# A four-layer image network on one core: moving layer 3's tile copies off GpSimd, shifting its gate chain, and reordering the loads at the start

## The chip, the core and the metric

The kernel runs on one core of a Trainium2 chip. The metric is the time of one execution in microseconds on the device, from its start to its end, as the median of several runs. A core has five engines that run side by side, each through its own queue of instructions in order: TensorE (PE, matrix products; its weight loads are listed as PEld), VectorE (DVE), ScalarE (ACT), GpSimd (POOL) and SyncE (SP, which here only issues transfers). ACT's queue issues transfers as well. SBUF is the working memory. Matrix products land in PSUM[...].

## The reference, cut to what matters

The input `x` is (4, 256, 48, 48): four samples, 256 channels, 2304 pixels. Four layers are applied in turn.

```python
# layer 0: group norm of x, then attention with 8 heads of 64 over all 2304
#          pixels; q and k are normed to length 1, scale 10; x = x + w_out(o)
# layer 1: group norm; gate from max-pool, blur-pool and depthwise 11x3 / 3x11
#          convolutions; x = x + norm * gate
# layer 2: group norm; non-local block: theta, phi, g of 64 channels each,
#          y = softmax(theta^T phi) g; W y goes through a batch norm over all
#          four samples; x2 = x + that
# layer 3: group norm of x2 -> h
#          gate = sigmoid(W2 leaky(W1 mean(h)))        one number per channel
#          z = depthwise 3x3 convolution of (h * gate) + bias
#          x = x2 + leaky(instance_norm(z))                leaky: slope 0.01
```

All data is float32. Layer 3's batch norm needs statistics over all samples, so nothing of layer 3 can start before the last attention unit of layer 2 is done.

## The kernel before, in words

`usual_path` (L56 to L1885) does the whole network; a second path further down is a fallback that doesn't run. Three samples' `x` live in SBUF as tiles of 128 partitions x 2 halves of the channels (k = 0, 1) x 2304 pixels. Sample 0's `x` is parked in DRAM before layer 3 and shares the buffer of sample 1.

**Start.** `load_x` brings in the first sample. The transfers of small parameters are issued on ACT's queue (L121 to L148): the vectors `vec`, then eleven weights of layers 2 and 3 (`w2c`, `b2c`, `Ww`, `w1`, `w2`), then `wo`. Behind them on ACT stands a one-element Exp (L168), which makes ACT load its table. `gn(0, ..., first=True)` takes `bn_stats` of each 384-column slice on DVE (L194), and reduces over groups with matrix products against the constant `gmat` (L215, L225). A reciprocal square root is done on POOL (`rsqrt`, L179). `norms` folds the normalization into the projection weights: PE computes bias vectors (L549) and ACT scales the weights in two 128x384 operations (L556). `start` projects (L581).

**Attention.** `attend()` (L454) runs phases of units; a unit is a run of key tiles, with two score products (L290), an exponential on ACT (L296), and two value products (L310) in each slot. Other work is put into numbered slots by a `work` dictionary and by `others`, lists of closures that are spread over slots: `spread(work, closures, slots)`. At the end of a unit the row sums are made (L399), inverted (`reciprocal`, L404) and multiplied in. `note(u)` (L407) keeps extremes of the row sums, from which `judge` decides at the end whether the usual path's results can be used. In layer 2, `w_mul` (L1087) forms W y in PSUM and `bn_stats` (L1095, L1369) takes its statistics; `sample_means(b)` aggregates them for each sample (L1139) and `earlier(k)` merges the first three samples. The next sample's group norm and its six projection chunks (`project2`, L1035 to L1056) are also spread over slots, and follow the statistics there.

**Layer 3.** Here all five queues run in the order in which the code is written (`manual_schedule`, L1400). PSUM is split into one `w` tile of two banks and three `cv` tiles of two banks. The samples are taken in the order `SEQ = [1, 2, 3, 0]`; a tile is one sample's one channel half, so there are eight tiles, and each has six conv steps (slices of 384 pixels). A tile i passes through these stages:

- `w_product(i, c)` (L1449): PE forms W y for one third of the pixels, into a PSUM tile of two banks.
- `grow(i, c)` (L1502): DVE scales it, adds x, and writes x2 into a padded image (50 x 50 with a border). Two operations, one for each bank.
- `square(i, c)` (L1526): ACT sums the squares around the mean. `border(i)` (L1511, L1514): POOL fills the frame.
- `place(i, h, j, q, how)` (L1535): copies 32 channels of half an image (32x1298) into `shifted`, moved by one of the taps' offsets. Each half tile needs twelve of them. Eight cross partitions (`AWAY`) and go through SP's queue as transfers. Four (j = q) stay in their partitions and are copies on an engine: L1542 on ACT, L1544 on POOL, L1546 on DVE.
- `products` (L1659): PE's convolution, twelve matrix products in each step, with taps on 96 or 128 rows.
- `evict` (L1671) and `square` (L1682): ACT takes the results to SBUF with their sums. `moments`, `scales`, `shift` (L1690 to L1730): DVE makes scale and shift, with one `rsqrt` on POOL.
- `scale` (L1736, ACT), `leak` (L1742, DVE: leaky relu), `gain` (L1747, DVE: adds x2), `store` (L1753, SP). Each has three pieces of 768 pixels a tile.

The class `Chain` computes one sample's gate in nine small operations: `total` (L1579, DVE), `groups` (L1586, PE), `inverse` (L1590, DVE, then POOL), `pooled` (L1596, DVE), `first_layer` (L1601, PE), `hidden` (L1608, DVE), `second_layer` (L1615, PE), `gate` (L1622, ACT), `scaled` (L1626, DVE). Its three matrix products write into the same `w` tile as the x2 products.

The order is set by an event table: `at(t, rank, fn)` puts a closure at conv step t, and within a step closures go out in the order of their ranks (FRONT, CONV, PRODUCT, GROW, MID, EVICT, SMALL, MOMENTS, SQUARE, SCALE, LAST, PLACE, STORE). `put_before` places the products and grows of a tile in the steps t-12 to t-10, if its conv starts at t; `put_tile` places conv and what follows it; `put_chain(t, steps)` places a gate chain at offsets from t, the first step of a sample. The last tile's statistics are taken straight from PSUM, and its scale, leak and gain come after the table, together with the pieces that `late` has collected from the tile ahead of it.

## Time and profile before

| | us |
|---|---|
| median of three runs | 3552.23 |
| lowest, highest run | 3548.91, 3552.97 |
| the profiled execution | 3548.99 |
| its span, from the first to the last instruction | 3547.2 |
| first projection matmul (L581) | 18.02 |
| last layer-2 row sums (L399) | 3358.37 |
| first conv step of layer 3 (L1659) | 3387.28 |
| last DVE operation (L1747) | 3540.55 |

A profile's line gives the line of the program, the engine, the operation and `out<-in` with shapes. In a list of groups there follow the count, the busy time, the mean of one in nanoseconds, and the idle time ahead of it with what ended it ("12.0 <-DVE pad L1502" is 12.0 us of waiting that VectorE's writing of `pad` ended). In a timeline, each line begins with the start and the length in microseconds of a run of like instructions, and ends with the idle time ahead of it. One float32 matrix product of the program appears as two records. A view by windows gives, for stretches of time, how long each engine was busy in them.

From 3357 to 3541 us, the groups that the change touches are these:

| row | count | busy us | mean ns |
|---|---|---|---|
| L1659 PE conv | 1152 | 105.6 | 512 |
| L1542 ACT copy 32x1298 | 26 | 33.0 | 1269 |
| L1544 POOL copy 32x1298 | 39 | 54.2 | 1389 |
| L1502 DVE grow 128x384 from the w tile | 38 | 21.6 | 611 |
| L1747 DVE gain 128x768 | 24 | 28.0 | 1166 |
| L1742 DVE leak 128x768 | 24 | 25.4 | 1057 |
| L1449 PE x2 product to the w tile | 152 | 17.6 | 536 |

Ten more grow operations and 40 more product records work on cv tiles, at the start of layer 3.

### The profile page before, as it was taken

To read this page: it belongs to the slowest core of one execution; us is meant where nothing else is said; L and a number is where in the kernel's file an instruction comes from. 1 tells how busy PE (TensorE), PEld (TensorE's weight loads), DVE (VectorE), ACT (ScalarE), POOL (GpSimd) and SP (SyncE) were. 2 spreads that over 40 slices of the span, in tenths; PEclk is the share of its full clock that TensorE was granted. 3 is DMA by queue.
4 is the path that set the end of the run, shared out by engine and by line. 5 is a ranking of instruction groups with operands and counts; after the bars stand their busy time and mean duration, and the time that the engine had idled before them with its cause. 6 is when DMAs were issued, how large, how long until landed. Compare 5 with 4: busy or idle time off the path is not lost. (4 is left out here: it accounts for less than half of the span.)

```text
span 3547.2 us, 88373 instructions
## 1 busy us (share of the span) xinstructions
PE 3426.8 (97%) x37036; PEld 1727.0 (49%) x37036; DVE 2550.9 (72%) x3472; ACT 2380.1 (67%) x3847; POOL 818.5 (23%) x626
## 2 busy tenths in 40 slices
PE   8999999999999999999999999999999999898976
PEld 4554545554444444444444444444444445565422
DVE  3455555567788788687887886878878879655856
ACT  4665666665886796558867975579668755555476
POOL 2333333321101010000111001110100116665553
PEclk9999999999999999999999999999999999999988
DMA  2211111111111111221111111111111100000076
GB/s 94 48 26 22 26 22 26 22 26 22 22 26 22 26 22 26 56 45 21 26 20 26 21 26 22 26 22 26 22 22 22 22 8 6 6 7 6 4 187 186
DMA packets 121752, 116.61 MB, mean 33 GB/s; under 512 B 58832, under 2 KB 112704, under 8 KB 120576
## 3 DMA queue, kind: packets, MB, share of 16 engines
q1 hardware_dynamic: 118592, 108.70, 16.4%
q8 instruction: 292, 4.78, 0.6%
q10 hardware_dynamic: 2752, 2.17, 0.2%
q14 instruction: 116, 0.95, 0.1%
HBM read 56.99 MB, written 11.80 MB: 19 GB/s over the span
## 5 line engine op out<-in xcount | busy, mean ns | idle before, releaser
L296 ACT ACTIVATE pt<-sc 128x768 f32<-128x768 f32 x1944 | 1475.2, 811 | 729.7 <-PE sc L290 721.2
L336 DVE TENSOR_TENSOR acc<-acc,pt 128x768 f32<-128x768 f32 x1368 | 1368.9, 1001 | 172.9 <-ACT pt L296 72.8
L310 PE MATMUL av<-pt,v 64*64 64x384 f32 x13824 | 1274.7, 484 | 0.0
L290 PE MATMUL sc<-q,k 64*64 64x384 f32 x13824 | 1269.9, 482 | 0.5 <-ACT pt L296 0.5
L290 PEld LDWEIGHTS sc<-q,k 64*64 64x64 f32 x13824 | 525.2, 133 | 589.7 <-issue 543.4
L310 PEld LDWEIGHTS av<-pt,v 64*64 64x64 f32 x13824 | 518.0, 133 | 599.1 <-issue 566.0
L391 POOL TENSOR_TENSOR o<-o,rinv 128x384 f32<-128x384 f32 x95 | 114.6, 1206 | 1737.3 <-DMA rinv<-rinv 1737.3
L321 POOL TENSOR_TENSOR half<-pt 128x768 f32<-128x768 f32 x189 | 364.1, 1930 | 539.4 <-ACT pt L296 502.3
L336 DVE TENSOR_TENSOR acc<-acc,half 128x768 f32<-128x768 f32 x171 | 192.8, 1127 | 232.6 <-POOL half L321 231.6
L677 DVE SCALAR_TENSOR_TENSOR x<-pj,bo,x 128x384 f32<-128x384 f32 x192 | 118.4, 617 | 308.6 <-PE pj L664 307.2
L853 ACT ACTIVATE prod<-pd,wt 128x256 f32<-128x256 f32 x486 | 337.0, 764 | 0.2
L581 PE MATMUL pj<-xs,w 128*128 128x384 f32 (+1 forms) x720 | 275.4, 505 | 0.0
L581 PEld LDWEIGHTS pj<-xs,w 128*128 128x128 f32 x720 | 124.1, 189 | 127.9 <-issue 39.5
L310 PE MATMUL av<-pt,qv 64*64 64x384 f32 x1728 | 177.0, 498 | 0.0
L290 PE MATMUL sc<-qv,kd 64*64 64x384 f32 x1728 | 171.4, 485 | 2.4 <-ACT pt L296 2.4
L876 DVE TENSOR_REDUCE prod<-prod 128x256 f32<-128x1280 f32 x114 | 168.7, 1480 | 0.3 <-ACT prod L853 0.3
L664 PE MATMUL pj<-o,wo 128*128 128x384 f32 (+1 forms) x384 | 159.8, 499 | 5.7 <-issue 3.6
L612 PEld LDWEIGHTS pj<-w,xs 128*128 128x128 f32 x1080 | 134.5, 191 | 24.1 <-issue 1.2
L612 PE MATMUL pj<-w,xs 128*128 128x128 f32 x1080 | 134.9, 275 | 0.0
L387 POOL TENSOR_TENSOR o<-raw 128x384 f32<-128x384 f32 x95 | 124.4, 1309 | 43.3 <-ACT raw L383 43.2
L330 DVE TENSOR_TENSOR acc<-pt 128x768 f32<-128x768 f32 x99 | 115.5, 1166 | 26.1 <-ACT pt L296 26.1
L383 ACT COPY raw<-av 128x768 f32<-128x768 f32 x108 | 86.4, 800 | 48.0 <-PE av L310 45.6
(247 smaller groups left out, 2402.4 us busy)
## 6 DMA issues: line engine op xcount, KB each, us to landing
xs<-in_x_dram SPq DMA_DIRECT2D x90, 384.0 KB
sh<-pad SPq DMA_DIRECT2D x126, 162.2 KB
rinv<-rinv SPq DMA_DIRECT2D x208, 94.5 KB
out_dram<-x SPq DMA_DIRECT2D x24, 384.0 KB
l<-row SPq DMA_DIRECT2D x416, 1.5 KB
w<-in_wqkv_dram SPq DMA_DIRECT2D x32, 192.0 KB
x<-in_x_dram SPq DMA_DIRECT2D x4, 1152.0 KB
x<-in_x_dram SPq DMA_DIRECT2D x9, 384.0 KB
```

The lines of the kernel that those rows point to most:

```text
L290: nc.tensor.matmul(ps[c * D : (c + 1) * D, h, :SL], lhsT=u["of"]["k"][r, j0 : j0 + D], rhs=u["of"]["q"][r, u["qc"]], start=True, stop=True,)
L296: nc.scalar.activation(pt, ps[:, :, :SL], AF.Exp, scale=u["scale"])
L310: nc.tensor.matmul(u["av"][h * D : (h + 1) * D, half, :SL], lhsT=value(u, j, h)[r], rhs=pt[r, h, :], start=j == 0, stop=j == JB - 1,)
L321: nc.gpsimd.tensor_add(half, pts[0], pts[1])
L336: nc.vector.tensor_add(u["acc"], u["acc"], term)
L387: eng.tensor_add(u["sum"], u["raw"][:, 0, :], u["raw"][:, 1, :])
L581: nc.tensor.matmul(ps[:, :n], lhsT=at["w"][:, k, t, :], rhs=xs[s][:, k, :n], start=k == 0, stop=k == NK - 1,)
L612: nc.tensor.matmul(ps[:, i * P : (i + 1) * P], lhsT=xs[s][:, k, i * P : (i + 1) * P], rhs=at["w"][:, k, 2, :], start=k == 0, stop=k == NK - 1,
L664: nc.tensor.matmul(ps[:, :n], lhsT=wo[:, p, k * P : (k + 1) * P], rhs=o["o"][:, :n], start=True, stop=True,)
L677: nc.vector.scalar_tensor_tensor(xs, ps[:, :SL], pair["bo"][:, k : k + 1], xs, ALU.add, ALU.add)
L853: nc.scalar.activation(bufs[n % 3][:, :, min(n, 1) + i].rearrange("p (r c) -> p r c", c=AS), pd[:, PAD + dr : PAD + dr + AS, PAD + dc : PA ...
L876: nc.vector.tensor_reduce(to, bufs[n % 3][:, :, : min(n, 1) + len(taps)], AX.X, ALU.add)
```

## The change

1. **Start.** The one-element Exp comes right after `vec`'s load. The eleven weights of layers 2 and 3 become a list `later`; they are issued on SP's queue, one to a slot, in a phase of layer 0 (b, p = 1, 1), behind `load_taps`. The operation `nb1` moves behind the first group norm. `rehearse` issues matrix products of `gmat` with 160 columns of x whose results nobody reads: one beside each `bn_stats`, and 2, 4 and 1 more along the chain. The first weights are scaled in six 128x128 operations in place of two 128x384.
2. **Layer 2's statistics.** `sample_means(0)` and `(1)` move from the end of layer 2 into slots of earlier phases, with a hand-written merge (`merge_two`, `merge_three`) in place of `earlier(k)`.
3. **End of layer 2.** The last unit's row sums are copied to SBUF on ACT (`lrow`), and `note` reads that copy, at a later place (behind `centres`). `hum(out, n)` issues n unread matrix products of 128x128: 13 ahead of the last y products, 11 ahead of the means' matrix product, 5 and twice 3 behind it.
4. **Layer 3.** POOL makes no more copies in `spread_out`; the table `HERE` places four copies for each half tile: those of the first half on DVE (steps t-6 and t-5), those of the second on ACT twice (t-3) and DVE twice (t-3, t-2). In the first tile two ACT copies become DVE copies. The x2 products write to one lasting two-bank tile `w_all`; the gate chain's results go into the free columns of its second bank (`g_tile`). `GATE_AT` gives the step of each of the chain's nine operations: from -1 to 12 in the middle samples, 3 to 12 in the first, -2 to 6 in the last. What follows a tile's conv is placed 5 (k = 0) or 2 (k = 1) steps later, and leak and gain of k = 1 one more. Two of the three late pieces of the tile ahead of the last go back into the table, ahead of or beside the last steps, so that one is left.

```diff
+    warm = cpool.tile([P, 1], F32, name="warm")
+    nc.scalar.activation(warm, mhalf[:, 0:1], AF.Exp)
...
+    def rehearse(ps, x):
+        nc.tensor.matmul(ps[:, 0, :WARM], lhsT=gmat, rhs=x[:, :WARM], start=True, stop=True)
+    def hum(out, n):
+        for _ in range(n):
+            nc.tensor.matmul(out, lhsT=gmat, rhs=gmat, start=True, stop=True)
...
             fold(u, nc.vector)
-            sample_means(0)
+            row = xsp.tile([P, NK, SL + 1], F32, tag="xs", name="lrow")[:, 0, :SL]
+            nc.scalar.copy(row, ps[:, :SL])
         nc.vector.reciprocal(u["rinv"], ps[:, :SL])
-        u["l"] = ps
+        u["l"] = row if u.get("final") else ps
...
-            for k in range(NK):
-                nc.scalar.activation(
-                    w[:, k], w[:, k], AF.Identity, scale=norm["rs"][:, k : k + 1]
-                )
+            if direct:
+                rehearse(sc_tile(), X[b][:, 0, :])
+            for t in range(3) if direct else [slice(0, 3)]:
+                for k in range(NK):
+                    nc.scalar.activation(
+                        w[:, k, t], w[:, k, t], AF.Identity, scale=norm["rs"][:, k : k + 1]
+                    )
...
+            for s, (to, fr) in enumerate(later):
+                work.setdefault(s + len(SHIFT), []).append(
+                    lambda to=to, fr=fr: nc.sync.dma_start(to, fr)
+                )
...
+        if b == 1:
+            spread(work, [lambda: sample_means(0)], [17])
+        if b == 2:
+            spread(work, [lambda: sample_means(1), merge_two], [17, 19])
...
-            spread(work, [lambda k=k: earlier(k) for k in range(NK)], [25, 26])
+            spread(work, [lambda: sample_means(2), merge_three], [25, 26])
...
-    noted[0]()
-    for b in range(1, NX - 1):
-        sample_means(b)
...
-    sample_means(NX - 1)
...
+    w_all = ps_w.tile([P, 2, 512], F32, name="w3")
     def w_tile():
-        return ps_w.tile([P, 2, 512], F32, tag="w", name="w3")
+        return [w_all[:, 0, :SL], w_all[:, 1, :SL]]
+    def g_tile():
+        return w_all[:, 1, SL:]
...
-    ahead = [w_product(1, 0, w_tile())]
+    w_product(1, 0, ahead[0])
+    hum(g_tile(), 5)
...
-        for j in range(4):
-            place(i, h, j, j, "act" if h and j != 2 else "pool")
+    def keep_here(i, h, js, how):
+        for j in js:
+            place(i, h, j, j, how)
...
-            how |= {(0, 0): "act", (1, 1): "pool", (2, 2): "act", (3, 3): "pool"}
+            how |= {(0, 0): "dve", (1, 1): "pool", (2, 2): "dve", (3, 3): "pool"}
...
-            return [
-                (-2, MID, total), (-1, SMALL, groups), (0, FRONT, inverse), (1, MID, pooled),
-                (3, SMALL, first_layer), (4, MID, hidden),
-                (5, SMALL, second_layer), (6, FRONT, gate), (7, FRONT, scaled),
-            ]
+            return [(t, *step) for t, step in zip(GATE_AT[self.n], steps)]
...
+    GATE_AT = {
+        0: (3, 4, 5, 5, 8, 9, 10, 11, 12), B - 1: (-2, -1, 0, 0, 2, 3, 4, 5, 6),
+    }
+    for n in range(1, B - 1):
+        GATE_AT[n] = (-1, 2, 4, 4, 8, 9, 10, 11, 12)
...
     spread_first(1)
     centres()
+    noted[0]()
...
         if c + 1 < L2C:
-            ahead.append(w_product(1, c + 1, cv_tile()))
+            ahead.append(w_product(1, c + 1, w_pair()))
+            hum(g_tile(), 3)
...
+    HERE = [
+        (-6, 0, (0, 1), "dve"), (-5, 0, (2, 3), "dve"),
+        (-3, 1, (0, 1), "act"), (-3, 1, (2,), "dve"), (-2, 1, (3,), "dve"),
+    ]
...
+        soon = t + 2 * NSL == T
+        t += 0 if soon else 2 if cv.k else 5
         at(t + 8, FRONT, cv.moments)
...
-            if soon and g:
+            if soon and g == NG3 - 1:
                 late.append((cv, g))
                 continue
...
-            at(t + 14, STORE, lambda k=cv.k: reload(k))
-    put_chain(7, judge())
+            at(t + 18, STORE, lambda k=cv.k: reload(k))
+    put_chain(14, judge())
```

## The prediction, made before the result was known

> **What bounds the kernel now.** I read the busy shares first, then the chain that ended last, then busy time by stretch, then waits and timelines at both ends of the stretches that the diff touches.

> ```profile
> PE 3426.8 (97%) x37036; PEld 1727.0 (49%) x37036; DVE 2550.9 (72%) x3472; ACT 2380.1 (67%) x3847; POOL 818.5 (23%) x626
> ...
> DVE x L1742 0%; DVE x L1747 0%
> ```

> Over the span TensorE (PE) is the bound, but the change hardly touches the 3200 us of attention that make up its 97%. The chain ends on layer 3's last VectorE (DVE) operations. So layer 3 gets its own rows, each sample being 12 conv steps:

> ```profile
> 3357.20:3387.28 30.08, 11.38 (x72) 4.21 (x72) 20.60 (x55) 13.35 (x18) 14.44 (x12) 0.68 0.38 92
> 3387.28:3419.84 32.56, 32.56 (x347) 11.32 (x346) 13.20 (x38) 21.38 (x38) 14.97 (x16) 0.92 0.62 152
> 3419.84:3458.09 38.25, 32.37 (x350) 11.15 (x346) 26.58 (x54) 30.57 (x51) 18.16 (x17) 0.96 0.80 228
> 3458.09:3497.22 39.13, 33.88 (x351) 11.35 (x347) 26.40 (x54) 31.17 (x53) 18.00 (x17) 0.91 0.84 231
> 3497.22:3540.55 43.33, 25.24 (x302) 10.24 (x298) 33.63 (x62) 24.76 (x37) 9.62 (x9) 0.86 0.52 166
> ```

> The columns are window, length, then busy PE, weight load, DVE, ScalarE (ACT), GpSimd (POOL), clock, DMA share and GB/s. In the first row, the passage from layer 2, PE works for 11 of 30 us. In rows 3 and 4 no engine fills the 38 to 39 us: a sample needs only about 30.3 on PE (six conv steps of 1.98, six of 2.88 with an x2 product, 1.1 of gate matmuls). The rest is chains of waits:

> ```profile
> 3425.09 0.88 PE L1449 MATMUL w<-y,Ww 64*64 64x384 f32 x8 [2.79 <-DVE gn_gv L1590]
> 3425.89 3.73 PE L1659 MATMUL cv<-sh,taps 96*32 96x384 f32 x24
> ...
> 3444.70 0.88 PE L1449 MATMUL w<-y,Ww 64*64 64x384 f32 x8 [2.34 <-ACT ga L1622]
> 3445.51 2.14 PE L1659 MATMUL cv<-sh,taps 96*32 96x384 f32 x24
> ```

> An x2 product (L1449) waits for the gate chain, which shares its PSUM tile; after the first wait the conv step takes 3.73 instead of 2.14. The next sample has such waits of 3.06 and 2.19, and steps of 3.3 and 3.7 behind them. The start has idle time too:

> ```profile
> 12.72 0.56 PE L215 MATMUL pj<-gn_mv,gmat 128*128 128x2 f32 x2 [12.72 <-DVE gn_mv L204]
> ...
> 18.02 2.92 PE L581 MATMUL pj<-x,w 128*128 128x384 f32 x4 [1.07 <-ACT w L556]
> 20.74 0.85 PE L587 MATMUL pj<-gn_nm,w 128*128 128x1 f32 x4
> 21.45 2.40 PE L581 MATMUL pj<-x,w 128*128 128x384 f32 x4
> ```

> A group of four such projection records takes 1.31 from 24.05 on; here it takes 2.92 and 2.40.

> **Lead-in.** Before, the scalar queue issues eleven layer-2/3 weight loads from 5.42 to 15.34[...], and the table load behind them runs 15.97–17.25; weight scaling follows at 17.37, projection at 18.02. After, the table load is done in the first microseconds and the eleven loads go on SP's queue in an attention phase, where SP is nearly idle and the tensors are needed 1000 us later: nothing, or at worst 0.5 us each of issue (as on ACT now) ahead of attention's own small transfers on SP, which have a whole attention unit of slack. The nb1 operation that made DVE wait 1.15 at 9.71 is moved behind the chain, and x no longer shares its DMAs: bn_stats ends at about 10.9 instead of 12.18 (-1.3). The first of six 128x128 scalings (some 0.3 instead of 0.55) releases the projection: the three steps behind the rsqrt (.16+.3+.1) bring it to about 15.0, 3.0 earlier. The unread 128x160 matmuls cost about .27 or .53 each (160/384 of .655 per call, or twice that) and lie in front of nothing as long as they keep pace with bn_stats at .48 each. If they warm PE, the first two groups take 3.3 instead of 6.03 (-2.7). Bounds for this part: -2.5 (they stay cold and stand once in the way) to -5.7; I take **-5.2**.

> [...] The profile's clock column shows 1.00 throughout this stretch, so only durations tell that PE is slow. [...] 2.79 and 2.19 were followed by slow steps, 2.34 was not. [...] by the rows they cost up to 1.7 more. I follow the rows, at half.

> **End of layer 2.** Sample means move into earlier phases (VectorE slack there; .3 each), but they occupy slots, and the last sample's norm and projections start two slots later. Now PE stalls .98 and 3.17 (3238.22, 3242.72, both on bst) and then runs 5.30 of attention where 3.0 is normal: 9.8 us where about 3.4 would do. Two slots of room (5.6 us) remove most: -5. In exchange the six projection chunks, now in pairs spaced by attention work (6.18 a pair, 18.5), run in one row: 5x3.4+2.8=19.8, +1.3; DVE additions 0 to 2, I take 1.4. Sum **-2.3**, between +1 (the stall only moves) and -5.

> **Passage to layer 3.** The new ACT copy of the row sum shares the PSUM bank with the reciprocal (2.56), which waits for it (a 128x384 copy is half of the 0.80 of L383's 128x768, and a handover): +.55. Behind it on DVE stand the two operations that make y, and PE's last products wait for those, so it is on the path. Removed from DVE there: note (1.1) and three sample_means (1.4), but PE waits for y anyway. Thirteen unread 128x128 matmuls (.23 warm, .45 cold) ahead of the y products make these 2.84 → about 1.9; aggregation is shorter by .45. Eleven more stand before the means matmul: 2.5 us. So that matmul is due at about 3371.5 against 3371.15: no gain yet. Then two tile copies (2x.83) and note (1.1) stand on DVE before the first grow of the second half, 3376.5 → 3380.0. PE idles there some 5 us[...]. The gate chain no longer stands before the convs (its 11.0 wait at L1586 goes), and the first conv needs the copies and the border only: about 3383.9 against 3387.28, with 1 us of cold work instead of 2.5, but 1.2 more of gate matmuls and handovers between the convs: 31.5+1 → first sample done at 3416.4 against 3419.84: **-3.4**.

> **A layer-3 sample.** Five POOL copies and one ACT copy per tile go; six DVE copies come. The trace has the DVE copy once:

> ```profile
> L1546 DVE COPY sh<-pad 32x1298 f32<-32x1298 f32 x1 | 0.8, 828 | 0.1
> L1544 POOL COPY sh<-pad 32x1298 f32<-32x1298 f32 x39 | 54.2, 1389 | 20.4 <-PE cv L1659 14.6 <-ACT junk L1526 3.6 <-DVE pad L1502 0.5
> ```

> DVE: 23.1 of work (six grow pairs, six leak/gain pairs of 1.92, two moment sets, chain) plus 12x.83=9.9: 32.9. Check from the row: 26.6 less about 3.2 that two-input operations lost beside POOL's copies (gain 1.02 → 1.90, leak .96 → 1.77) plus 9.9 is 33.2. ACT falls to about 28, PE stays 30.3. So DVE is the bound with 33; 38.7 now. But the gate chain is written in the product's other bank, behind grows: PE's group matmul (step 2) waits about 2.2 and its first layer (step 8) about 3.7 for a grow that DVE reaches late behind its copies. Behind each wait PE's next conv step is queued, and ACT's evictions wait for that; no row of before shows these two waits, the nearest are the 2.2 to 3.1 above, and they may be nothing if DVE keeps up. DVE in turn waits about 2.7 at the start of the next sample. That makes a period of 36.4, and 0.8 of half clock: 37.2. Two samples: 2x(38.7-37.2) = **-3.0**. If no grow is late it is 33 (-11 over the two); if each stalls at the longest now seen and half clock follows, 40 (+3).

> [...] the POOL pair beside the DVE copy took 3.24 instead of 2x1.26. POOL keeps only rsqrts and border copies. The gate's rsqrt has DVE waiting for it, so no copy is running; the others would lose at most .83 each, four per sample, off the path. [...] by the rows nothing on the end: I take nothing.

> **Last sample.** It has six leak/gain pairs less one behind the final statistics: four pairs of 1.92 remain in place of five (-1.9), and its gate is six to eight steps earlier (-.5): **-2.4**. The stores after DVE's end keep their 6.7.

> **Sum.** 5.2+2.3+3.4+3.0+2.4 = 16.3. The profiled run took 3548.99 (span 3547.2 and 1.8 around it) → 3532.7; the median of the runs lies 3.24 higher: 3552.23-16.3 = **3535.9**. About 0.2% (7.1 us) is what a measurement of this kernel can tell from no change.

> **Rivals.**
> A, DVE's floor is reached (0.22): grows are not late, samples take 33.0–33.5, conv starts at 3379. For: ACT and PE have slack, POOL contention is gone. Against: bank-shared waits. -16.3-8-4 gives 3524.
> B, DVE takes the place of the gate wait (0.17): each late grow stalls PE over 3 us and at half clock; the period stays 39–40 and the eleven matmuls delay the means. For: 3.73 behind 2.79; DVE 85% loaded. Passage gains nothing, the three middle samples lose 4.6, and the ends keep 5.2+2.3+2.4: 5.3 in all, 3546.9, within 0.2%.
> C, slower (0.05): the copies on DVE are dearer than the single one seen. 32 of them fall on samples in which they bound; -16.3+32(x-.83) is zero at x=1.34 and +7.1 at 1.56; at 1.7, 3564. For: DVE operations did double beside POOL's copies. Against: those copies are gone, and .83 was measured beside one.
> D, the warming does nothing (0.08): unread matmuls keep their cost, lead-in and passage lose 5: 3541.
> The forecast itself has 0.48.

> **Chances.** Over 0.2% faster (below 3545.1): forecast, A, D and a third of B, 0.83. Same: the rest of B, with edges, 0.12. Slower 0.05. The range holds A's 3524 with its own 2 us and B's 3547.

> **What would show it.** First L581 at about 15.0 with groups of 1.3; no stall on bst near 3238; conv 3.4 earlier; windows by sample about 37.2 with DVE over 30 busy, POOL about 4; waits of PE for pad L1558 of 2 to 4 us; some 45 DVE copies at .83; four pairs in the tail. Wrong if copies exceed 1.0, if samples stay at 39, or if L581 is still at 2.9.

## The result, and the profile after

The changed kernel's median is 3540.47 us (8 runs, 3536.92 to 3541.88), against 3550.48 for the kernel before in the same measurement (8 runs). The ratio is 0.9969, with a 95% interval of 0.9958 to 0.998. It is 10.0 us faster, 0.31%. The forecast was 16.3 us, to 3536. The profiled execution took 3540.24, with a span of 3538.5; before it was 3548.99 and 3547.2.

The span is 8.66 us shorter by the two profiles. The table cuts both at the same events (starts of instructions in the timelines; for the last VectorE operation, its end), and sets the prediction's terms beside them. The batch norm over all samples that layer 3 has to wait for is layer 2's.

| part | before | after | change | forecast |
|---|---|---|---|---|
| start to the third projection group | 24.05 | 18.27 | -5.8 | -5.2 |
| attention and the rest, up to the end of layer 2's first sample | 2999.65 | 3005.16 | +5.5 | 0 |
| layer 2, samples 2 to 4, to the last row sums | 334.67 | 328.65 | -6.0 | -2.3 |
| last row sums to the first conv step | 28.91 | 28.81 | -0.1 | } -3.4 |
| layer 3, sample 1 (12 conv steps) | 32.88 | 32.62 | -0.3 | } |
| samples 2 and 3 | 77.37 | 80.20 | +2.8 | -3.0 |
| last sample, to the last VectorE operation | 43.02 | 40.20 | -2.8 | -2.4 |
| last stores | 6.62 | 4.61 | -2.0 | 0 |

The start, in TensorE's timeline of the changed kernel (start, length, and the idle time ahead in brackets):

```profile
5.14 5.99 PE L190 MATMUL sc<-x,gmat 128*128 128x160 f32 x24 [5.14 <-DMA x<-in_x_dram]
...
14.88 1.45 PE L604 MATMUL pj<-x,w 128*128 128x384 f32 x4
...
16.53 1.54 PE L604 MATMUL pj<-x,w 128*128 128x384 f32 x4
...
18.27 13.15 PE L604 MATMUL pj<-x,w 128*128 128x384 f32 x40
```

The first row is the unread products; they fill 6 of the 12.7 us in which TensorE had stood still. The groups of four that took 2.92 and 2.40 take 1.45 and 1.54, and the first one starts at 14.88 instead of 18.02.

The stretches of the changed kernel that answer to the five of before (busy PE, weight load, DVE, ACT, POOL, clock, DMA share, GB/s); the first is the passage, then come the four samples:

```profile
3352.08:3380.89 28.81, 17.99 (x141) 12.03 (x141) 22.09 (x47) 9.66 (x15) 16.19 (x14) 0.85 0.35 82
3380.89:3413.51 32.62, 31.35 (x348) 12.17 (x351) 18.48 (x36) 21.89 (x41) 1.70 (x5) 0.97 0.67 165
3413.51:3454.43 40.92, 33.90 (x353) 12.75 (x349) 32.78 (x70) 28.18 (x49) 4.06 (x7) 0.92 0.75 205
3454.43:3493.71 39.28, 32.68 (x352) 14.88 (x344) 32.17 (x66) 28.31 (x50) 2.96 (x5) 0.96 0.85 241
3493.71:3533.91 40.20, 24.56 (x297) 9.81 (x296) 37.03 (x80) 21.18 (x32) 2.88 (x5) 0.86 0.55 177
```

VectorE now works 32 to 33 us in each middle sample, ScalarE 28, GpSimd 3 to 4: the loads are those that were forecast. Yet these samples take 40.9 and 39.3 us. Where that goes is in TensorE's timeline:

```profile
3424.84 0.38 PE L1645 MATMUL w<-gn_sq,gmat 128*128 128x2 f32 x2 [2.12 <-DVE pad L1558]
...
3444.58 0.59 PE L1660 MATMUL w<-pm,w 128*64 128x1 f32 x4 [3.77 <-DVE pad L1558]
3445.10 6.90 PE L1719 MATMUL cv<-sh,taps 96*32 96x384 f32 x48
```

Two matrix products of the gate chain wait 2.12 and 3.77 us for VectorE's grow; behind the longer wait two conv steps take 6.90, where 4.08 is usual.

### The profile page after: what moved, and what is told of

It is laid out like the page before. It is cut to its first block, busy times and chain, and to the rows that moved or that the text cites. A ratio compares the mean times of both kernels' runs of the same rounds, so it can differ in the third digit from the quotient of the medians.

```text
span 3538.5 us, 88557 instructions
## 1 busy us (share of the span) xinstructions
PE 3439.1 (97%) x37144; PEld 1743.7 (49%) x37144; DVE 2567.9 (73%) x3523; ACT 2369.3 (67%) x3843; POOL 774.9 (22%) x591
## 3 DMA queue, kind: packets, MB, share of 16 engines
q1 hardware_dynamic: 120240, 109.16, 16.3%
## 5 line engine op out<-in xcount | busy, mean ns | idle before, releaser
L355 DVE TENSOR_TENSOR acc<-acc,half 128x768 f32<-128x768 f32 x171 | 184.1, 1076 | 216.6 <-POOL half L340 216.0
L349 DVE TENSOR_TENSOR acc<-pt 128x768 f32<-128x768 f32 x99 | 112.8, 1140 | 39.8 <-ACT pt L315 39.8
```

Source lines behind the costliest of these rows:

```text
L355: nc.vector.tensor_add(u["acc"], u["acc"], term)
```

## The experiments

Each of the twelve was measured beside the kernel before. Their parts of layer 3, in us, cut as above (the conv step called 12 in the expectations, which count from 0, is called step 13 here):

| run | ratio to before (interval) | passage | sample 1 | 2 | 3 | last |
|---|---|---|---|---|---|---|
| before | | 28.9 | 32.9 | 38.3 | 39.1 | 43.0 |
| changed | 0.9969 (0.9958 to 0.998) | 28.8 | 32.6 | 40.9 | 39.3 | 40.2 |
| e_noreh | 0.9978 (0.997 to 0.9986) | 28.8 | 32.3 | 40.7 | 39.2 | 40.2 |
| e_slots | 0.9984 (0.9978 to 0.9991) | 28.8 | 32.4 | 40.7 | 39.2 | 40.2 |
| e_copies | 0.9999 (0.999 to 1.0007) | 28.9 | 34.7 | 39.0 | 39.9 | 41.0 |
| e_pool | 0.9954 (0.994 to 0.9967) | 28.8 | 32.0 | 35.1 | 35.3 | 42.9 |
| e_gate9 | 0.9971 (0.996 to 0.9981) | 28.8 | 30.6 | 39.3 | 42.0 | 40.7 |
| e_memset | 0.9967 (0.9955 to 0.9979) | 29.5 | 31.8 | 39.8 | 39.1 | 40.2 |
| e_first | 0.9955 (0.9942 to 0.9969) | 26.0 | 31.8 | 39.9 | 39.3 | 40.2 |
| e_nohum | 0.9947 (0.9933 to 0.996) | 19.0 | 36.0 | 39.7 | 38.6 | 40.2 |
| e_hum3 | 0.9946 (0.9933 to 0.996) | 19.1 | 35.1 | 38.1 | 40.3 | 40.2 |
| e_mix | 0.9933 (0.992 to 0.9947) | 26.1 | 31.9 | 35.1 | 35.3 | 40.2 |
| e_best | 0.9934 (0.9921 to 0.9948) | 20.3 | 35.6 | 36.6 | 35.3 | 40.3 |
| e_best2 | 0.9928 (0.9914 to 0.9941) | 20.3 | 35.6 | 35.1 | 35.3 | 40.3 |

**The start, with and without warming.** The results of the products left out are read by nobody.

```diff
     def rehearse(ps, x):
-        nc.tensor.matmul(ps[:, 0, :WARM], lhsT=gmat, rhs=x[:, :WARM], start=True, stop=True)
+        pass
```

> The changed kernel without its 19 unread 128x160 products in the lead-in (rehearse does nothing); the reordered loads stay. Theory 1 (the lead-in's gain has two halves, an earlier table load and a warm TensorE): the first projection still starts near 15.2, but its first two groups take 3.4 and 2.6 again instead of 1.65 and 1.74, the first record of full clock moves from 10.2 to about 20, and everything after is 2.5 to 3 us later: median near 3543. Rival (the order of the loads alone gives the gain, the slow groups came from transfers that ran beside them): groups of 1.7 as in the changed kernel, no later than 0.3 us.

TensorE's timeline of this run:

```profile
15.36 2.91 PE L604 MATMUL pj<-x,w 128*128 128x384 f32 x4
...
18.78 2.09 PE L604 MATMUL pj<-x,w 128*128 128x384 f32 x4
```

The groups are slow again (2.91 and 2.09 in place of 1.45 and 1.54), and the third one begins at 21.07: 2.8 later than in the changed kernel, 3.0 earlier than before. The clock record begins with an entry of full clock: at 23.2 us before and at 10.2 in the changed kernel. (The views print 1.00 ahead of that entry for want of a record.) So the 5.8 us are 3.0 from the order of the loads and 2.8 from the unread products, with which TensorE runs the two groups faster. By the ratios the kernel loses 0.09% of 3550, 3.2 us. Theory 1 holds.

**Layer 2's statistics.** The slots as before, in the changed kernel:

```diff
-        if b == 1:
-            spread(work, [lambda: sample_means(0)], [17])
-        if b == 2:
-            spread(work, [lambda: sample_means(1), merge_two], [17, 19])
...
-            spread(work, [lambda: sample_means(2), merge_three], [25, 26])
+            spread(work, [lambda k=k: earlier(k) for k in range(NK)], [25, 26])
...
     last_y = [w_mul(B - 1, k, L2C - 1, wide=True) for k in range(NK)]
+    for b in range(NX):
+        sample_means(b)
```

> The changed kernel with layer 2's statistics as before the change (merged late, nothing in slots 17 and 19 of the two middle samples, sample means of the first three at the end). Theory 1 (moving them gave about 5 in the attention of layer 2, which the profile of the changed kernel lost again to half-clock stretches in places where the program was not changed): the second sample's attention of layer 2 takes 139 instead of 133.5 to 135.8, the third's 112.7 instead of 110.4 to 111.3, the last's 82.9 instead of 83.9; median 4 to 6 above the changed kernel, if the clock's stretches elsewhere are alike. Rival (the gain there is the clock's phase, not the slots): 134 to 136 and 110.4 again, median within 2.5.

The median is 3545.26 (before in the same measurement 3550.36): by the ratios 5.3 us above the changed kernel. Layer 2's four samples in the windows of this run, then of the changed kernel:

```profile
2903.26:3018.39 115.13, 106.25 (x1172) 58.72 (x1168) 98.98 (x114) 62.42 (x100) 74.57 (x40) 1.00 0.06 5
3018.39:3156.91 138.52, 127.39 (x1517) 81.59 (x1513) 82.32 (x100) 73.69 (x131) 87.31 (x49) 0.96 0.06 6
3156.91:3269.67 112.76, 103.20 (x1088) 59.37 (x1084) 69.57 (x79) 60.45 (x95) 70.74 (x38) 0.95 0.07 7
3269.67:3353.13 83.46, 79.96 (x952) 44.07 (x944) 67.12 (x80) 44.51 (x60) 42.53 (x40) 1.00 0.04 4
```

```profile
2904.90:3023.43 118.53, 111.17 (x1172) 59.20 (x1168) 95.23 (x114) 62.47 (x101) 73.39 (x40) 0.96 0.05 5
3023.43:3156.93 133.50, 122.36 (x1469) 77.47 (x1465) 77.07 (x98) 72.28 (x127) 85.60 (x47) 0.97 0.07 6
3156.93:3268.19 111.26, 103.08 (x1136) 63.81 (x1132) 71.36 (x90) 61.75 (x99) 73.76 (x40) 0.97 0.08 7
3268.19:3352.08 83.89, 79.96 (x953) 44.06 (x945) 67.75 (x83) 44.52 (x60) 42.58 (x40) 1.00 0.04 4
```

With the old slots samples 2 to 4 of the layer take 334.7 together, as in the kernel before (334.7); with the new ones they took 328.5 to 330.1 in the eleven profiles that have them. (48 records of work also moved from the second sample to the third, so only the sum is to be compared.) The gain of 4.6 to 6.2 us is the slots', and theory 1 holds. Part of it comes through the clock: with the old slots six half-clock stretches of 3.4 us fall in these three samples (counted in the clock record of the kernel before; the clock column above gives six for e_slots too), with the new ones four (clock record of the changed kernel). At 1.1 us each (the first sample, below, loses 3.4 by three of them), two fewer are an estimated 2.2 us. The first sample, whose program is the same in both, is the other half of the expectation: 115.13 at clock 1.00 here, 118.53 at 0.96 in the changed kernel. The run e_copies, whose attention is that of the kernel before, has 118.50 there, and the kernel before 115.18. So this loss belongs to the single execution.

**Copies, alone and undone.** One part alone, in the kernel before:

```diff
-        for j in range(4):
-            place(i, h, j, j, "act" if h and j != 2 else "pool")
...
+            for dt, h, js, how in HERE:
+                at(t + dt, PLACE, lambda i=i, h=h, js=js, how=how: keep_here(i, h, js, how))
```

> The kernel before with one part of the change alone: for tiles 1 to 7 the copies within a partition go to VectorE (six a tile) and ScalarE (two) at the steps of the change; the old gate steps, post-processing, passage and lead-in stay. Theory 1 (the copies on VectorE are what costs, the later post-processing is what gives): samples 2 and 3 get longer than 38.3 and 39.1 by 2 to 5 each, median 3553 to 3560. Rival (copies off GpSimd are a gain in the old table too, since two-input operations of VectorE no longer stretch): 36 to 38, median 3543 to 3548.

No difference in the median (3550.34 to 3549.46). Samples 1 to 3 are longer, by 1.8, 0.7 and 0.8; the last is 2.0 shorter. Neither theory had that; the copies cost less than 2 a sample in the old table. Its 43 VectorE copies have a mean of 828 ns (the 45 of the changed kernel 898, with the slow pair shown below), so rival C's price can be struck out.

The same part undone for tiles 1 to 7, in the changed kernel:

```diff
     HERE = [
-        (-6, 0, (0, 1), "dve"), (-5, 0, (2, 3), "dve"),
-        (-3, 1, (0, 1), "act"), (-3, 1, (2,), "dve"), (-2, 1, (3,), "dve"),
+        (-6, 0, (0, 1, 2, 3), "pool"), (-3, 1, (0, 1, 3), "act"), (-3, 1, (2,), "pool"),
     ]
```

> The changed kernel with the within-partition copies of layer 3 given back to GpSimd and ScalarE as before the change (five and three a tile); the new gate steps and later post-processing stay. Theory 1 (the copies on VectorE hold up the grows, and these TensorE): the waits of TensorE for pad at groups and first_layer, 2.1 and 3.8, fall under 1; VectorE has 10 us less a sample but loses 3 beside GpSimd's copies; samples of 34 to 37 instead of 40.9 and 39.3, median near 3533. Rival (the new step table is what stalls, whoever copies; GpSimd copies of 1.39 with transfers behind them are late for the conv): stalls of 2 and more stay at the same places, samples of 38 and more, median 3539 to 3544.

Theory 1 holds, though the two waits do not fall under 1. The middle samples of this run, in the same columns:

```profile
3414.77:3449.87 35.10, 30.67 (x353) 14.66 (x349) 26.17 (x58) 30.59 (x51) 17.69 (x17) 1.00 0.77 215
3449.87:3485.20 35.33, 31.08 (x352) 14.94 (x344) 24.50 (x54) 30.69 (x53) 17.52 (x17) 1.00 0.96 279
```

VectorE has 6.6 to 7.7 us less to do, GpSimd 14 more, and TensorE runs at clock 1.00. Its waits for pad at the two gate products are 1.3 and 1.4 in place of 2.1 and 3.8, and no other wait for pad is above 1.8. The new step table with the old copies is 3.2 and 3.8 faster than before in these samples, and the copies on VectorE take 5.8 and 4.0 away. Only in the last sample, where VectorE has no grows to do, are they worth having (40.2 against 42.9; e_mix below has them there alone and takes 40.2 too).

**More room for the gate's products.**

```diff
-        0: (3, 4, 5, 5, 8, 9, 10, 11, 12), B - 1: (-2, -1, 0, 0, 2, 3, 4, 5, 6),
+        0: (3, 4, 5, 5, 9, 10, 10, 11, 12), B - 1: (-2, -1, 0, 0, 2, 3, 4, 5, 6),
...
-        GATE_AT[n] = (-1, 2, 4, 4, 8, 9, 10, 11, 12)
+        GATE_AT[n] = (-1, 3, 4, 4, 9, 10, 10, 11, 12)
```

> The changed kernel with two matrix products of the gate chain one conv step later in samples 1 to 3 of the order (groups at 3 instead of 2, first_layer at 9 instead of 8). Theory 1 (these two stand on TensorE's queue ahead of the next conv step and wait for the third grow in their bank; a step more is cover for it): the stall of 2.12 at groups goes, that of 3.77 at first_layer falls to about 1.8, the half-clock conv steps behind it (6.90 and 5.65 for two) become 4.1 to 5, and the two middle samples go from 40.9 and 39.3 to 36 to 37: median 6 to 9 us lower, near 3533. Rival (VectorE with its twelve copies a sample is the bound, the stalls only show it): the waiting moves to the next products and conv steps, the samples stay above 38.5, median within 3 us of the changed kernel.

The stall at groups is gone and that at first_layer falls to 1.7, as theory 1 said, but the gain doesn't come: 2.3 appear at an x2 product of sample 3 (L1504 for pad), 2.6 and 1.7 at second_layer, and both samples still have slow conv steps behind such waits: two take 5.77 in sample 2, where 4.08 is usual; in sample 3, at another place, two take 3.07 and 4.07, where 2.14 each is usual. The samples are 39.3 and 42.0. The rival holds: late grows find another place to stall TensorE. Giving VectorE less (e_pool) helped; giving the waits more room didn't.

**The passage: GpSimd, VectorE and the unread products.** First the memsets:

```diff
-    nc.gpsimd.memset(shifted[0][0:32, 2:4, :], 0.0)
+    for sh in shifted:
+        nc.gpsimd.memset(sh[0:32, 2:4, :], 0.0)
...
-    for sh in shifted[1:]:
-        nc.gpsimd.memset(sh[0:32, 2:4, :], 0.0)
```

> The changed kernel with the two memsets of 32x2600 on GpSimd moved ahead, to the place of the first one, where GpSimd has nothing to do. Theory 1 (the two VectorE copies that took 4.83 us at 3368.73 were held back by GpSimd's memsets and copies beside them, and TensorE's idle 8.17 us behind them grew by that): the pair of copies falls to between 1.7 and 2.5, the idle stretch of TensorE to about 5.5, and the first conv step comes 2 to 3 us earlier; median near 3538. Rival (the copies wait for something else, or the first conv step is set by GpSimd's own copies and the transfers): the pair may shorten, but the first conv step moves by less than 0.7.

What VectorE and GpSimd did in the passage of the changed kernel:

```profile
3368.73 4.83 DVE L1602 COPY sh<-pad 32x1298 f32<-32x1298 f32 x2
3373.57 0.17 DVE L1548 TENSOR_TENSOR minus<-bi,means 128x8 f32<-128x8 f32 x1
```

```profile
3366.74 3.24 POOL L1600 COPY sh<-pad 32x1298 f32<-32x1298 f32 x2 [0.47 <-DVE pad L1558]
3370.03 5.73 POOL L1856 MEMSET sh<- 32x2600 f32 x2
```

And in e_memset:

```profile
3367.30 3.74 DVE L1603 COPY sh<-pad 32x1298 f32<-32x1298 f32 x2
3371.05 1.13 DVE L1549 TENSOR_TENSOR minus<-bi,means 128x8 f32<-128x8 f32 x1
```

Two VectorE copies took 4.83 beside GpSimd's copy and memsets; another pair, with no copy or memset of GpSimd beside it, took 1.66 (at 3385.78, changed kernel). GpSimd's memsets took longer too, 5.73 in place of the 4.46 of the kernel before. Without the memsets beside them the two copies still took 3.74; GpSimd's copies, moved up, ran at that time. What the pair gained, 1.1, the small operation behind it lost again: it took 1.13 in place of 0.17 and ended with GpSimd's last copy, at 3372.2. So the rival holds for the memsets (TensorE's wait stayed, 8.5), and the cause was only half named: VectorE's pair is slow beside GpSimd's copies alone as well (3.74 against 1.66).

Then the copies too:

```diff
-            how |= {(0, 0): "dve", (1, 1): "pool", (2, 2): "dve", (3, 3): "pool"}
+            how |= {(0, 0): "act", (1, 1): "pool", (2, 2): "act", (3, 3): "pool"}
```

> The changed kernel with the two memsets moved ahead as in the run before and, beyond that, the first tile's two VectorE copies of the second half given back to ScalarE. Theory 1 (VectorE stands still behind GpSimd's copies while TensorE waits for the grow behind them; with the memsets moved the pair still took 3.74 beside GpSimd's copies): from the last row sums to the first conv step 28.8 becomes 24.5 to 26, the idle 8.2 to 8.5 of TensorE 4 to 5.5; median near 3537. Rival (the first conv step is set by the transfers and by GpSimd's copies of the first tile, whoever works before them): 28 or more, TensorE waits for something other than pad.

The passage takes 26.0 and TensorE's wait is 4.9: theory 1, at the upper end of its range. So the two VectorE copies, and the memsets at their old place, had cost 2.8 of the passage. But 4.9 were left, before a product nobody reads. That is what the next two runs are about. Both leave out unread products only:

```diff
     def hum(out, n):
-        for _ in range(n):
-            nc.tensor.matmul(out, lhsT=gmat, rhs=gmat, start=True, stop=True)
+        pass
```

> The changed kernel without the 35 unread 128x128 products between the layers (hum does nothing); the lead-in's stay. Theory 1 (they warm TensorE for the y products but stand on the path of nothing that ends last, since the first conv step waits for VectorE): the y products take 2.8 and 4.1 instead of 1.5 and 2.2, the means' product comes within 1 us of where it was, the first conv step less than 1.5 later, first conv steps slower by 1 to 2: from the last row sums to step 12 61.4 becomes 61 to 64, median 3540 to 3543. Rival (the eleven products ahead of the means delay it): the means' product and the first conv step come 1.5 to 2.5 earlier.

The first conv step comes 9.8 us earlier in the passage, and the first sample takes 3.4 longer: neither theory, and four times what the rival allowed. So the next run took out only two of the groups:

```diff
             ahead.append(w_product(1, c + 1, w_pair()))
-            hum(g_tile(), 3)
```

> The changed kernel without the two groups of three unread products that stand between the x2 products of the second tile, right ahead of the first conv step; the 13, 11 and 5 stay. Theory 1 (these six write the bank that VectorE's grow of that tile reads last, so they hold TensorE back until grow is done, though the conv behind them doesn't need it): from the last row sums to the first conv step 28.8 becomes 19 to 21 as without any of them, TensorE stays warm enough that the first conv step takes 2 to 4, and step 12 is reached in 52 to 55 instead of 61.4: median near 3532, or below. Rival (what held TensorE was the eleven ahead of the means, or the cold first steps give the time back): 25 or more to the first conv step, or 58 and more to step 12.

TensorE at the first conv step, in the changed kernel and then in e_hum3:

```profile
3376.24 1.65 PE L195 MATMUL w<-gmat 128*128 128x128 f32 x6 [8.17 <-DVE pad L1558]
3377.82 1.56 PE L1504 MATMUL cv<-y,Ww 64*64 64x384 f32 x8
3379.31 1.65 PE L195 MATMUL w<-gmat 128*128 128x128 f32 x6
3380.89 2.96 PE L1719 MATMUL cv<-sh,taps 96*32 96x384 f32 x24
```

```profile
3364.67 0.88 PE L1504 MATMUL cv<-y,Ww 64*64 64x384 f32 x8 [0.25 <-DVE pad L1558]
3367.49 4.78 PE L1719 MATMUL cv<-sh,taps 96*32 96x384 f32 x24 [1.94 <-DMA sh<-pad]
```

Theory 1 holds: the first three unread products wait 8.17 us for a grow that the conv behind them does not need. They write free columns of the bank that this grow reads. Without them the passage is 19.1, and from the row sums to step 13 it is 54.2 in place of 61.4. The median is 3531.93 (before in the same measurement 3550.36).

**Put together.** e_mix joins e_first and e_pool (whose table is HERE now) and keeps the change's VectorE copies, in THERE, for the last tile alone; e_best takes the two groups of unread products out of that, e_best2 the eleven ahead of the means too.

```diff
+            for dt, h, js, how in THERE if i == len(TILES) - 1 else HERE:
```

> The changed kernel with: the passage of the run e_first; GpSimd and ScalarE copies (five and three a tile) for tiles 1 to 6 as in the run e_pool; VectorE copies as in the change for the last tile alone. If the parts are as they looked one by one: passage 24.5 to 26, samples 32, 35.1, 35.3, last sample 40.2 to 42.8; median 3528 to 3533. If the samples' gain came only from the clock's phase, samples 2 and 3 are back at 38 or more and the median above 3536.

> The run e_mix (memsets ahead, first copies on ScalarE, GpSimd copies for tiles 1 to 6) without the two groups of three unread products. If the gains add: from the last row sums to step 12 58.0 becomes 51 to 54, samples 2 and 3 35.1 and 35.3, median 3521 to 3525, below both kernels. If the earlier first conv step only meets VectorE and ScalarE still busy with the first tiles: 56 to 58, median 3527 to 3529.

> The run e_best without the eleven unread products ahead of the means' product too (13 and 5 stay). Theory 1 (the eleven delay the means' product, and with it the frame and the first copies, by 1.5): step 12 comes 1 to 2 earlier than in e_best. Rival (without them TensorE is cold at the first conv steps): the same or up to 3 later.

e_mix is what the parts had promised (3528.57 against 3549.46). e_best brings the first conv step 5.8 earlier but gives 3.7 of it back in the first sample: from the row sums to step 13 it takes 55.9, between the two cases. Its ratio can't be told from that of e_mix. e_best2 has the same 55.9: theory 1 fails, and the time is the rival's ("the same"). Its cause, a cold TensorE, isn't shown, though: the time did not get longer without the eleven. So they neither delay nor speed up anything that counts. At 3525.94 (3550.36 before) it is the fastest of all, 0.72% faster than the kernel before and 0.4% faster than the change by the ratios. Its lead over e_best lies within their intervals.

## Why the prediction was right, and where its sum was not

The direction and the range were right; the sum was 16.3 and 10.0 came. That it came so near is in part luck. By the profiles, the passage, the first and the two middle samples were forecast to give 6.4 and lost 2.4, and the attention lost 5.5 by what no term held; layer 2 (3.7), the stores (2.0), the lead-in (0.6) and the last sample (0.4) gave 6.7 more than forecast.

*Lead-in* (5.2): right, 5.8, and each half was right too (3.0 and 2.7 forecast for the earlier start and the warm groups; e_noreh measured 3.0 and 2.8). That the unread products make the groups behind them faster was the author's estimate, for which the trace of before had no row; e_noreh shows it (1.45 and 1.54 with them, 2.91 and 2.09 without).

*End of layer 2* (2.3): mis-sized, the slots give about 5.3. The stalls of .98 and 3.17 went as forecast, and a new one of 4.09 came in place of the 2.89 for acc; TensorE before, and then in the changed kernel:

```profile
3201.26 1.56 PE L343 MATMUL pj<-acc,ones 64*64 64x384 f32 x8 [2.89 <-DVE acc L336]
...
3238.22 1.33 PE L1087 MATMUL pj<-y,Ww 64*64 64x384 f32 x8 [0.98 <-DVE bst L1095]
...
3242.72 1.01 PE L999 MATMUL pj<-gn_nb,w2c 128*128 128x1 f32 x4 [3.17 <-DVE bst L1095]
```

```profile
3206.05 2.01 PE L1112 MATMUL pj<-y,Ww 64*64 64x384 f32 x8 [4.09 <-DVE bst L1120]
```

Samples 2 and 3, which hold the stalls and the six chunks in one row, got 7.0 shorter in the profile (-5+1.3 forecast), and the fourth 1.0 longer. So the gain was taken too small, and "DVE additions 0 to 2, I take 1.4" too large; how the 7.0 divide between the stalls, the row and the clock stays open.

*Passage* (3.4): it gave 0.1, and 0.4 with the first sample. The term that failed is "two tile copies (2x.83)": they took 4.83, 3.2 more, and e_first, without them and with the memsets moved, has 2.8 of it back. GpSimd was copying and clearing at that time, and the rows above show what VectorE's pair took beside it: 4.83, then 3.74 without memsets, against 1.66 alone. How the two engines hold each other up, the runs don't show. The prediction weighed only what GpSimd could lose in the steady samples, where it is nearly idle, and not what VectorE could lose at the one place where both copy at once. The forecast also had the path to the first conv step wrong. The 11.0 wait at the gate chain went, as forecast. The text said that the first conv "needs the copies and the border only", yet its sum let TensorE idle ahead of it for the grow ("some 5 us"), which only the unread products needed. They waited 8.17, and e_hum3 shows that 9.7 us of the passage hang on them, 7.3 after what the first sample gives back.

*The middle samples* (3.0): they lose 2.8, and "samples stay at 39" was the prediction's own sign of being wrong. The loads and both stalls were right to 0.1 (2.2 and 3.7 forecast). What was too small is "0.8 of half clock" and waits not counted at all. (The period of 36.4 is also more than the named terms give: 30.3+2.2+3.7 = 36.2.) In sample 2 the half clock behind 3.77 costs 6.90-4.08 = 2.8; three short waits (0.46, 0.21 and 0.30, two of them at x2 products) add 1.0: 30.3+2.1+3.8+2.8+1.0 = 40.0 of the 40.9 measured. In sample 3 the half clock costs 5.65-4.08 = 1.6. Rival B, a chance of 0.17, was right about these samples and about the passage, though not by the eleven products that it blamed (e_best2); its total of 5.3 was too low, layer 2 and the stores giving 5.7 more.

```profile
3422.89:3426.30 3.41, 1.21 (x16) 0.42 (x20) 2.32 (x4) 3.38 (x7) 1.12 (x2) 1.00 0.96 251
3426.30:3429.71 3.41, 3.41 (x28) 0.91 (x24) 3.38 (x4) 1.37 (x5) 3.29 (x3) 0.50 0.49 158
```

The changed kernel has its 2.12 spread over the first two of these, and its 3.77 in the third:

```profile
3420.14:3423.55 3.41, 2.12 (x24) 0.47 (x16) 3.29 (x10) 1.73 (x3) 0.55 (x1) 1.00 0.43 102
3423.55:3426.96 3.41, 2.12 (x26) 1.65 (x30) 3.33 (x8) 3.22 (x7) 0.00 (x0) 1.00 1.01 251
3440.62:3444.03 3.41, 0.18 (x4) 0.00 (x0) 3.33 (x5) 1.39 (x4) 0.00 (x0) 1.00 0.45 99
3444.03:3447.44 3.41, 2.86 (x20) 1.30 (x24) 3.34 (x6) 2.80 (x4) 0.00 (x0) 0.50 0.92 268
```

From the first conv step on, in these two traces, the stretches at full clock that half clock followed had TensorE busy for 0.00 to 1.26 us of the 3.41, and those that full clock followed for 1.73 or more. So a stall of some 2 to 3 us was followed by half clock where nearly all of it lay in one such stretch (2.79, 2.19), and not where it was spread over two (2.12, 2.34).

*Last sample* (2.4): right, 2.8. Four pairs stand behind the final statistics in place of five (7.8 us against 9.7), and these come 0.9 earlier in the sample (0.5 forecast). It needed the VectorE copies, though: with GpSimd's (e_pool) the pairs are four too, but the statistics come later and the sample takes 42.9. *Stores* (0): 2.0 shorter. In all runs the stretch behind VectorE's end is 4.6 to 5.2, also in e_copies, whose tail is written as before; why the kernel before had 6.6 stays open.

*What no term covered*: the attention that the change leaves nearly alone took 5.5 us longer in the changed kernel's profile, 3.4 of it in the first sample of layer 2. The first two such places, each with the 3.4 us ahead of it:

```profile
2880.80:2884.20 3.40, 2.20 (x15) 1.74 (x15) 0.78 (x3) 1.86 (x4) 0.00 (x0) 1.00 0.02 5
2884.20:2887.60 3.40, 3.40 (x18) 1.14 (x22) 2.38 (x7) 0.00 (x0) 0.00 (x0) 0.51 0.00 0
...
2911.60:2915.00 3.40, 1.97 (x6) 0.81 (x6) 2.60 (x8) 0.92 (x2) 0.69 (x2) 0.99 0.00 0
2915.00:2918.40 3.40, 3.40 (x25) 1.34 (x28) 2.39 (x2) 0.00 (x0) 1.78 (x2) 0.50 0.00 0
```

TensorE is busy for all of a 3.4 us stretch, at half clock, and had been idle for 1.2 or 1.4 us of the one ahead. The kernel before has no half clock ahead of 3054.25, and e_slots, whose program is the same up to there, shows a clock of 1.00 over layer 2's first sample.

## What to carry to other kernels

An operation that only warms an engine is an instruction like any other: before placing it, look at which buffer it writes and who reads that last, for the next real work is queued behind it (here for 8.17 us). When copies are moved to an engine that is not the bound, ask what else on that engine others wait for; here the grows were late, and a wait of 3.8 us cost TensorE another 1.6 to 2.8 in half clock. A loss or gain that two profiles show in an unchanged stretch should be looked for in a third before it is explained.

## What the runs showed that was not expected

In the attention, the traces of the kernel before and of the changed one have stretches of 3.4 or 6.8 us at half clock while TensorE is busy for 2.3 to 3.4 us of every 3.41. Each follows a stretch with some idle time, but often little: TensorE was busy in it for 0.28 to 2.85 us of the 3.41, while one with 1.40 (from 3047.42, before) was followed by full clock. What decides there stays open. Layer 2's first sample takes 115.13 us in e_slots, at clock 1.00, and 118.53 in the changed kernel, the same program there, with three such stretches. Cases that differ in layer 3 alone reached the last row sums anywhere between 3347.4 and 3354.0. A change of a few microseconds in a kernel like this is better read from its own stretch of the timeline than from the end time.
